# Two bottleneck blocks on one core: rows of the 3x3 stage's first group later, bias on ScalarE, streams without a unit of look-ahead, more idle matmuls

## The chip, the cores and the metric

The kernel runs on one core of a Trainium2 chip. The metric is the device time of one execution in microseconds (us). Three executions of the kernel before took 1949.6, 1950.11 and 1950.57 us; the median, 1950.11 us, is what the change is compared with.

## The reference

Two residual bottleneck blocks, one after the other, on x of 64 images, 1024 channels, 14 x 14 pixels, all float32. One block is

```
out = relu(bn(conv1x1(x,   w1, b1), g1, be1))      # 1024 -> 256 channels
out = relu(bn(conv3x3(out, w2, b2), g2, be2))      # 256 -> 256, padding 1
out = bn(conv1x1(out, w3, b3), g3, be3)            # 256 -> 1024
out = relu(x + softplus(residual_scale) * out)
```

`bn` takes mean and variance of its own input over images and pixels. So each convolution has to be complete, as far as its statistics go, before what follows it can be scaled, and this cuts the kernel into stages.

## The kernel before

**Stages.** In the trace they stand as follows. First 1x1 convolution of block 0: to 304 us. 3x3 convolution of block 0: 305 to 589. Statistics of the last 1x1 convolution from a Gram matrix (`gram`): 589 to 672. A fused stage, last convolution of block 0 beside first of block 1 (`fused`): to 1270. 3x3 of block 1: 1271 to 1556. Its Gram matrix: to 1640. Last convolution of block 1 (`final`): to the end at 1951.

**Streams of 1x1 convolutions.** A 1x1 convolution is cut into units, each a seven-product scheme for a 2 x 2 block product (`class Seven`, methods `p1` to `p7`, each followed by `after1` to `after7`, which take the result out of PSUM). `stream` (line 300) yields the products in the order p1 of this unit, p3 and p4 of the unit before (`last`), then p6, p2, p5, p7. It keeps one unit in hand: `following = next(items, None)` at the top of the loop makes the next unit while this one is only starting. Making a unit has effects, since the generators that yield units also load x, make the sums that the products need, and send rows out. In `final.pairs` (lines 1157 to 1170) a pair of x tiles has four units (q = 0 to 3). At q = 0 `column_sums` makes four sums t3, t2, t1, t4 on VectorE (lines 430 to 433; t1 and t2 have one buffer each, t3 and t4 two). After each unit the unit two back goes out: `go_out` (line 520) does one row on VectorE (line 522) and starts two transfers on SyncE's queue (line 525). After q = 1 the next two x tiles are loaded on the same queue (line 123) into a pool of five tiles. `Conv3.add` (line 466) adds a product to x on VectorE. p3 accumulates into the bank that p5 wrote, so it must wait until `after5`'s add of line 466 has read that bank.

**The 3x3 stage.** `conv2` (line 556) works in eight groups of eight images. Rows are combined first (VectorE makes combinations of input rows: `combine`, lines 658 to 723), then per combination columns are combined and multiplied. A group has six combinations in the pairs (1, 2), (3, 4), (5, 0); I number them as items 0 to 47, so item 6 opens the second group. An item needs from VectorE `sums` (line 624), `v` (line 630) and `diffs` (line 640), each made once for a pair, and has on TensorE, in the order of the loop at line 963: `m` from `sums` (`start`), the odd half of the `columns` of the item before, `l` from `diffs` (`middle`), the even half of its own `columns` from `v`. ScalarE copies m into the `columns` banks (lines 758 and 760) and l into `ls` (line 768). `outputs` adds `columns` and `ls` on VectorE (line 801). The very first item has no m; its bias comes in by four scalar_tensor_tensor operations in `add_to` (line 799). `finish` (line 811) is a generator that is sent every finished item: after the fourth item of a group it makes `c` and `e` (lines 835, 836) and writes the group's output rows: six operations of `stt` (line 593) and one add (line 843). In group 0 `begin` (line 901) then takes a mean of some rows as the centre of later moments (lines 905 to 908). The item three ahead is made only after `finish` was sent the current one.

**What sets the order.** The text is traced once. A planner lays down each engine's instructions by when they can run in its own simulated time; among those that can run, the one traced earlier goes first. It reaches far ahead for what is ready: the t3 of line 430 at 1706.25 us is traced at the start of the unit that runs at about 1719. `keep_in_program_order` pins an instruction behind the one traced just before it on its engine; all matmuls, ScalarE's `act` calls and line 522 are pinned. [...]

**Idle matmuls.** `busy` (line 170) issues matmuls of 448 columns whose result nobody reads; six of them stand at the end of each 3x3 stage (line 979), ahead of the Gram stage's first transposes (`by_tensor`, line 1030).

Of the kernel before, what the change touches and what calls it, by code (L numbers as in the profile page):

```python
# [87 lines left out]
def bottlenecks(ctx: ExitStack, tc: tile.TileContext, x, w1s, w2s, w3s, pars, out):  # L88
# [81 lines left out]
    def busy(psum, tag, n, with_=None):  # L170

        v = ident if with_ is None else with_
        for i in range(n):
            matmul(psum.tile(448, tag), v, v[:, :1].to_broadcast([P, 448]), start=True, stop=True)
# [122 lines left out]
            yield from self.p3()  # L297
            yield from self.p4()

    def stream(items, beside=lambda: None):  # L300


        before, items = None, iter(items)
        now = next(items)
        while now is not None:
            following = next(items, None)
            yield from now.p1()
            if before is not None:
                beside()
                yield from before.last()  # L310
                beside()
            else:
                yield from now.p2()
            yield from now.p6()
            if before is not None:
                before.end()
                if following is not None:
                    beside()
                    yield from now.p2()
            beside()  # L320
            yield from now.p5()
            beside()
            yield from now.p7()
            beside()
            if following is None:
                yield from now.p2()
            before, now = now, following
        yield from before.last()
        before.end()

# [225 lines left out]
    def conv2(psum, pool, b, par, aff, affine_of, stats):  # L556
# [35 lines left out]
        def stt(to, a, by, c):  # L592
            return nc.vector.scalar_tensor_tensor(to, a, by, c, ALU.mult, ALU.add)
# [131 lines left out]
        class Products:  # L725
# [36 lines left out]
            def middle(self):  # L762

                l = self.whole("l", DIFF, self.diffs)
                ls = pool.tile([P, 2 * MS * RT * GI * WH], FP, tag="ls", name="ls", bufs=BUFS["ls"])
                self.ls = ls[:, : 2 * MS * self.n].rearrange("p (q o n) -> p q o n", q=2, o=MS)
                for q, sign in (EVEN, 1.0), (ODD, -1.0):
                    nc.scalar.activation(self.ls[:, q], l, AF.Copy, scale=sign)

            def columns(self, *qs):  # L770
                parts = {ODD: [(D3M1, self.r[:, :, :, WH:])], EVEN: [(D0M2, self.r[:, :, :, :WH])]}
# [20 lines left out]
            def add_to(self, f):  # L792

                to, v, ls = halves(f), self.by_columns(self.banks), self.by_columns(self.ls)
                if self.first:
                    for q, o in itertools.product((EVEN, ODD), range(MS)):
                        one = [w[:, q].rearrange("p (o l) c -> p o l c", o=MS)[:, o] for w in (to, v, ls)]
                        bias = par[:, B2 + o : B2 + o + 1]
                        nc.vector.scalar_tensor_tensor(one[0], one[1], bias, one[2], ALU.add, ALU.add)
                else:  # L800
                    nc.vector.tensor_add(to, v, ls)  # L801
                return f

        def halves(f):
# [3 lines left out]
        def outputs(c):  # L808
            return c.add_to(new("f", c.lines // GI))

        def finish():


            for g in range(NG):
# [9 lines left out]

                ca = yield
                fa = outputs(ca)
                fb = outputs((yield))
                a, d = new("fa"), new("fb")
                nc.vector.tensor_add(a, fa, fb)
# [11 lines left out]
                if by_transfer:  # L841

                    nc.vector.tensor_add(out_rows[0][:, :, :full], a3, c)
                    nc.scalar.activation(out_rows[0][:, :, full], a[:, :, full], AF.Copy)
                else:
                    nc.vector.tensor_add(a3, a3, c)
                end = y_grp[:, :, g, H - 1]
                if by_transfer:

                    for o in range(MS):  # L850
                        stt(out_rows[3][:, o], e[:, o], 8.0, d3[:, o])
                    nc.scalar.activation(end, d[:, :, full], AF.Copy)
                else:
                    stt(d3, e, 8.0, d3)
# [108 lines left out]
        for k in range(NG * NF):  # L963
# [25 lines left out]
    def gram(psum, pool, homes, aff, minus_c, beside):  # L989
# [162 lines left out]
    def final(psum, pool, xpool, xs, a, w3, aff):  # L1152


        units = []

        def pairs():
            for t in range(1, T - 1, 2):
                ys = [[two(t + i, s) for i in range(2)] for s in range(MS)]
                sums = column_sums(pool, ys, PX)  # L1160
                for q in range(CS // 2):
                    units.append(Conv3Pair(psum, pool, xs[t : t + 2], q, PX, ys, sums, w3, aff, out[t : t + 2]))
                    yield units[-1]
# [12 lines left out]
        residual(psum, xs[T - 1], 1, T - 1, a, aff)  # L1176

    def fused(psum, pool, xpool, xs, w1, w3, aff, par, stats, one_done):
# [17 lines left out]
        a, c = stream(first_convs()), stream(last_convs())  # L1196
        for i in range(LAG):
            next(c)
        while True:
# [125 lines left out]
    with tc.tile_pool(name="first", bufs=1) as one, tc.tile_pool(  # L1325
# [35 lines left out]
        for _ in stream(items(), beside):  # L1361
            pass

    for b in range(2):
# [95 lines left out]
```

## Time and profile before

| | us |
|---|---|
| median of three executions | 1950.11 |
| the profiled execution | 1952.81 |
| its span, first to last instruction | 1951.0 |
| TensorE busy in the span (matmuls) | 1918.5 |
| VectorE busy | 1541.4 |
| ScalarE busy | 1044.6 |
| GpSimd busy | 577.1 |

The profiled execution is 1.8 us longer than its span and 2.7 us longer than the median. Busy times of TensorE are of matmuls that overlap in a pipeline. By stage, VectorE was busy 12 to 17 of 20 us in the first stage, 19 to 20 of 20 us in the 3x3 stages, 13 to 15 of 20 in the fused stage and about 16 of 20 in the last one; TensorE shows 20.00 of 20 us nearly throughout, but for the joints of the stages, one gap in each 3x3 stage and a small gap in every pair of the last stage.

### The profile page before, as it was taken

The page shows a single profiled execution, that of the slowest core. Times are in us where ns is not written, and L with a number is a line of the kernel's source. Part 1 is how long each engine was busy: PE and PEld are TensorE (multiplying, and loading weights), DVE is VectorE, ACT ScalarE, POOL GpSimd, SP SyncE. Part 2 cuts the span into 40 slices and gives each one's busy share as a digit, 9 for nine tenths or more (in the row PEclk, how much of TensorE's full clock was granted, in tenths as well). Part 3 has the DMA queues.
Part 4 walks back from the last instruction along what each step waited for, and adds up shares of the span by engine and source line. Part 5 has one row for each costly group of instructions (what it writes and reads, how often), then busy time and mean ns, then how long its engine had stood idle before and what let it go on. Part 6 is the DMA issues. An engine that isn't in the chain of part 4 may idle for free.

```text
span 1951.0 us, 27071 instructions
## 1 busy us (share of the span) xinstructions
PE 1918.5 (98%) x9430; PEld 1617.1 (83%) x9430; DVE 1541.4 (79%) x2479; ACT 1044.6 (54%) x2094; POOL 577.1 (30%) x674
## 2 busy tenths in 40 slices
PE   9999999999999999999999999989999999999998
PEld 5555558999997799999999999989999887555555
DVE  5778768999997667676776776699999975888786
ACT  2222214677765155555555555457777642666665
POOL 0111100212105133433433433201121061666664
PEclk9999999999999999999999999999999999999999
DMA  7777634787848534444444444268787386899997
GB/s 290 277 250 256 242 120 162 190 227 202 228 140 213 190 149 182 166 168 183 178 166 165 183 181 166 100 183 216 209 218 220 125 204 234 296 324 341 332 341 265
DMA packets 201849, 413.92 MB, mean 212 GB/s; under 512 B 37808, under 2 KB 178000, under 8 KB 185200
## 3 DMA queue, kind: packets, MB, share of 16 engines
q1 hardware_dynamic: 161728, 324.66, 48.8%
q0 software_dynamic: 34368, 36.45, 9.2%
q10 hardware_dynamic: 5616, 51.06, 6.3%
q8 instruction: 75, 1.23, 0.3%
q14 instruction: 62, 0.51, 0.1%
HBM read 263.75 MB, written 115.34 MB: 194 GB/s over the span
## 4 chain that ended last, share of the span: by engine, by line
PE 88%; DVE 5%; issue 5%; ACT 1%; POOL 1%; DMA 1%; SPq 0%; DVEq 0%; POOLq 0%; ACTq 0%
PE cy L168 16%; PE columns L168 14%; PE ay L168 14%; PE cp L168 12%; PE ap L168 9%; PE l L168 7%; PE m L168 7%; PE cx L168 4%; PE ax L168 4%; PE ps L168 1%; DVE x L466 1%; POOL u L215 1%; DVE ct L431 1%; DMA u<-y 0%; DVE ct L433 0%
## 5 line engine op out<-in xcount | busy, mean ns | idle before, releaser
L333 ACT ACTIVATE cu<-cy,scale 128x196 f32<-128x196 f32 (+1 forms) x552 | 257.7, 473 | 286.6 <-PE cy L168 280.0
L168 PE MATMUL columns<-v,ub 128*128 128x224 f32 (+1 forms) x1536 | 301.7, 338 | 0.0
L168 PEld LDWEIGHTS columns<-v,ub 128*128 128x128 f32 x1536 | 270.4, 189 | 3.1
L333 ACT ACTIVATE x<-x,shift 128x392 f32<-128x392 f32 x428 | 239.6, 612 | 55.4 <-POOL x L492 53.4
L466 DVE SCALAR_TENSOR_TENSOR x<-cp,scale,x 128x196 f32<-128x196 f32 (+1 forms) x368 | 178.3, 485 | 97.9 <-PE cp L168 96.3
L168 PE MATMUL cy<-ct,ws 128*128 128x196 f32 (+1 forms) x736 | 221.9, 383 | 1.1 <-ACT cu L333 1.1
L487 POOL TENSOR_TENSOR x<-x,cu 128x196 f32<-128x196 f32 (+1 forms) x184 | 158.9, 864 | 173.9 <-ACT cu L333 162.4
L168 PE MATMUL ay<-at,ws 128*128 128x196 f32 (+1 forms) x752 | 209.1, 381 | 0.0
L492 POOL TENSOR_TENSOR x<-x,cu 128x392 f32<-128x392 f32 x124 | 125.9, 1015 | 193.2 <-DVE x L466 183.5
L168 PEld LDWEIGHTS ay<-at,ws 128*128 128x128 f32 x752 | 136.5, 190 | 33.4
L168 PEld LDWEIGHTS cy<-ct,ws 128*128 128x128 f32 x736 | 133.4, 190 | 36.4 <-ACT cu L333 3.8
L168 PE MATMUL m<-sums,ua 128*128 128x224 f32 (+1 forms) x752 | 148.3, 341 | 5.4 <-DVE sums L624 5.4
L513 POOL TENSOR_TENSOR x<-x,cu 128x392 f32<-128x392 f32 x120 | 124.5, 1039 | 86.1 <-DVE x L466 65.4
L168 PE MATMUL l<-diffs,ub 128*128 128x224 f32 (+1 forms) x768 | 148.9, 337 | 0.0
L168 PEld LDWEIGHTS m<-sums,ua 128*128 128x128 f32 x752 | 132.9, 191 | 7.2 <-DVE sums L624 6.5
L333 ACT ACTIVATE au<-ay 128x196 f32<-128x196 f32 (+1 forms) x141 | 53.7, 381 | 156.0 <-PE ay L168 153.2
L466 DVE SCALAR_TENSOR_TENSOR x<-cx,scale,x 128x196 f32<-128x196 f32 (+1 forms) x184 | 89.4, 486 | 59.0 <-PE cx L168 57.9
L168 PEld LDWEIGHTS l<-diffs,ub 128*128 128x128 f32 x768 | 134.5, 189 | 0.8 <-issue 0.4
L867 POOL DMA_DIRECT2D y<-f x24 | 30.9, 1529 | 349.5 <-DVE f L801 309.0
L168 PE MATMUL cx<-y,w 128*128 128x196 f32 (+1 forms) x404 | 124.1, 392 | 0.4 <-DVE x L1141 0.4
L168 PE MATMUL cy<-y,w 128*128 128x196 f32 (+1 forms) x404 | 123.8, 392 | 0.0
L168 PE MATMUL cp<-zt 128*128 128x257 f32 x392 | 118.9, 385 | 1.7 <-DVE zt L1041 1.7
(214 smaller groups left out, 4001.7 us busy)
## 6 DMA issues: line engine op xcount, KB each, us to landing
x<-in_x SPq DMA_DIRECT2D x62, 1568.0 KB, 6.8
ub<-u SPq DMA_DIRECT2D x94, 768.0 KB, 5.4
x<-mid SPq DMA_DIRECT2D x32, 1568.0 KB, 8.6
mid<-x ACTq DMA_DIRECT2D x31, 1568.0 KB, 5.1
out<-x SPq DMA_DIRECT2D x123, 392.0 KB, 6.6
ua<-u SPq DMA_DIRECT2D x94, 256.0 KB, 3.0
u<-y POOLq DMA_DIRECT2D x48, 256.0 KB, 6.1
home<-y SPq DMA_DIRECT2D x90, 96.0 KB, 4.2
```

Of the source, the lines that this page charges most:

```text
L168: tc.keep_in_program_order(nc.tensor.matmul(*args, **kw))
L215: nc.gpsimd.dma_start(out=us[b][i][:, s, o], in_=u)
L333: tc.keep_in_program_order(nc.scalar.activation(*args, **kw))
L431: nc.vector.tensor_add(t2, t3, ys[0][0])
L466: nc.vector.scalar_tensor_tensor(v, bank, self.scale[:, o : o + 1], v, ALU.mult, ALU.add)
L487: nc.gpsimd.tensor_add(self.part(1, 1), self.part(1, 1), u3)
L492: nc.gpsimd.tensor_add(v, v, self.u12)
L513: nc.gpsimd.tensor_add(v, v, self.u12[:, i * self.n : (i + 1) * self.n])
L867: nc.gpsimd.dma_start(out=out_rows[3][:, o], in_=fa[:, o, :full], accum_op=ALU.add)
```

## The change

Six edits. In code:

```diff
-    def stream(items, beside=lambda: None):
-        before, items = None, iter(items)
-        now = next(items)
-        while now is not None:
-            following = next(items, None)
+    def stream(items, total, beside=lambda: None):
+        before = None
+        for k, now in enumerate(items, 1):
             yield from now.p1()
...
-                if following is not None:
+                if k < total:
                     beside()
                     yield from now.p2()
...
-            if following is None:
+            if k == total:
                 yield from now.p2()
-            before, now = now, following
+            before = now
...
                 for q, sign in (EVEN, 1.0), (ODD, -1.0):
-                    nc.scalar.activation(self.ls[:, q], l, AF.Copy, scale=sign)
+                    if self.first:
+                        for o in range(MS):
+                            bias = par[:, B2 + o : B2 + o + 1]
+                            nc.scalar.activation(self.ls[:, q, o], l[:, o], AF.Identity, bias=bias, scale=sign)
+                    else:
+                        nc.scalar.activation(self.ls[:, q], l, AF.Copy, scale=sign)
...
-                if self.first:
-                    for q, o in itertools.product((EVEN, ODD), range(MS)):
...
-                        nc.vector.scalar_tensor_tensor(one[0], one[1], bias, one[2], ALU.add, ALU.add)
-                else:
-                    nc.vector.tensor_add(to, v, ls)
+                nc.vector.tensor_add(to, v, ls)
...
                 fa = outputs(ca)
+                if g == 1:
+                    begin(y_grp[:, :, 0, 1 : 4 * full : 4, :])
...
-                for o in range(MS):
-                    stt(out_rows[1][:, o, :full], e[:, o], 2.0, d3[:, o])
-                    stt(out_rows[2][:, o], c[:, o], 4.0, a3[:, o])
...
-                if g == 0:
-                    begin(out_rows[1][:, :, :full])
+                def complete():
...
+                if g:
+                    complete()
...
                 fa = outputs((yield))
+                if g == 0:
+                    complete()
...
-        busy(psum, "m", 6)
+        busy(psum, "m", 7)
...
                 yield by_tensor(a if a < head else a + STEP)
+                if i == 0:
+                    busy(psum, "ax", 1)
...
-        for _ in stream(pairs()):
+        for _ in stream(pairs(), (T // 2 - 1) * CS // 2):
```

`complete` holds the row operations of lines 838 to 854, unchanged. A unit is now made when its turn comes, that is, after p7 of the unit before; the other calls of `stream` get their number of units in the same way. The row operations of group 0 stand after the outputs of the group's fifth item; in the other groups they stay. The first item's bias goes into `ls` by four activations instead of two. The centre is made in group 1, after the outputs of item 6, from the same rows of group 0.

More of the change, by code (lines that the diff above doesn't have):

```diff
@@ L794, in add_to @@
                 to, v, ls = halves(f), self.by_columns(self.banks), self.by_columns(self.ls)
-                if self.first:
-                    for q, o in itertools.product((EVEN, ODD), range(MS)):
-                        one = [w[:, q].rearrange("p (o l) c -> p o l c", o=MS)[:, o] for w in (to, v, ls)]
-                        bias = par[:, B2 + o : B2 + o + 1]
-                        nc.vector.scalar_tensor_tensor(one[0], one[1], bias, one[2], ALU.add, ALU.add)
-                else:
-                    nc.vector.tensor_add(to, v, ls)
+                nc.vector.tensor_add(to, v, ls)
                 return f
@@ L837, in finish @@
                 a3, d3 = (v[:, :, :full] for v in (a, d))
-                for o in range(MS):
-                    stt(out_rows[1][:, o, :full], e[:, o], 2.0, d3[:, o])
-                    stt(out_rows[2][:, o], c[:, o], 4.0, a3[:, o])
[L841 to L846, printed above, removed]
                 end = y_grp[:, :, g, H - 1]
-                if by_transfer:
+                def complete():
                     for o in range(MS):
[L851 to L854, printed above, removed]
-                if g == 0:
-                    begin(out_rows[1][:, :, :full])
+                        stt(out_rows[1][:, o, :full], e[:, o], 2.0, d3[:, o])
+                        stt(out_rows[2][:, o], c[:, o], 4.0, a3[:, o])
+                    if by_transfer:
+                        nc.vector.tensor_add(out_rows[0][:, :, :full], a3, c)
+                        nc.scalar.activation(out_rows[0][:, :, full], a[:, :, full], AF.Copy)
+                    else:
+                        nc.vector.tensor_add(a3, a3, c)
+                    if by_transfer:
+                        for o in range(MS):
+                            stt(out_rows[3][:, o], e[:, o], 8.0, d3[:, o])
+                        nc.scalar.activation(end, d[:, :, full], AF.Copy)
+                    else:
+                        stt(d3, e, 8.0, d3)
+                if g:
+                    complete()
                 if last_group:
@@ L1194, in first_convs @@
                 yield Conv1(psum, pool, xs[t : t + 1], (t,), w1, par, stats, one_done)
-        a, c = stream(first_convs()), stream(last_convs())
+        a, c = stream(first_convs(), T), stream(last_convs(), (T - 1) * CS // 2)
         for i in range(LAG):
@@ L1359, in items @@
                 yield Conv1(psum, one, xs, (t, t + 1), w1, par[0], stats1, one_done)
-        for _ in stream(items(), beside):
+        for _ in stream(items(), T // 2 - 1, beside):
             pass
```

## The prediction

> **What bounds the kernel.** I read the page's first two parts, then the waits of TensorE, then the busy times of all engines in windows around each wait, and last the timeline there.
>
> ```profile
> span 1951.0 us, 27071 instructions
> PE 1918.5 (98%) x9430; PEld 1617.1 (83%) x9430; DVE 1541.4 (79%) x2479; ACT 1044.6 (54%) x2094; POOL 577.1 (30%) x674
> ...
> PE cp L168 <- DVE x L466: 7.0, 15, 0.9
> PE m L168 <- DVE sums L624: 5.4, 2, 2.7
> ```
>
> TensorE (PE) is the bound: 32.5 us of the span are without a matmul. The last two lines, from the waits (total, times, longest), are the largest of what VectorE causes. So a gain can only come from gaps of TensorE, or from stretches in which its clock is halved. The windows show those (columns: stretch, its length, busy us of PE, PEld, DVE, ACT, POOL, granted clock, DMA share, GB/s):
>
> ```profile
> 344.00:346.00 2.00, 0.00 (x0) 0.00 (x0) 2.00 (x4) 0.61 (x2) 0.80 (x1) 1.00 0.17 64
> 346.00:348.00 2.00, 1.98 (x7) 1.86 (x8) 2.00 (x2) 0.00 (x0) 2.00 (x3) 0.69 0.55 55
> 348.00:350.00 2.00, 2.00 (x7) 1.76 (x7) 2.00 (x2) 1.20 (x3) 1.06 (x1) 0.50 1.15 117
> ...
> 1558.00:1560.00 2.00, 2.00 (x9) 1.61 (x10) 1.85 (x3) 2.00 (x2) 0.00 (x0) 0.62 0.00 0
> 1560.00:1562.00 2.00, 2.00 (x10) 1.82 (x10) 1.21 (x2) 2.00 (x3) 0.23 (x1) 0.53 0.00 0
> ```
>
> VectorE is full while TensorE stands still at 344, and then the clock is 0.5. Three places are left to work out.
>
> **First, group 0 of the 3x3 stage.** The timeline (start, duration, engine, line):
>
> ```profile
> 338.57 0.51 DVE L593 SCALAR_TENSOR_TENSOR y<-fc,fa 128x336 f32<-128x336 f32 x1
> ...
> 341.85 0.92 DVE L905 BATCH_NORM_STATS2 first_stats<-y 128x6 f32<-128x336 f32 x2
> 342.68 0.18 DVE L907 BATCH_NORM_AGGREGATE mv_first<-first_stats 128x2 f32<-128x6 f32 x1
> 342.76 1.07 DVE L688 TENSOR_TENSOR r<-steps 128x896 f32<-128x896 f32 x1
> ...
> 344.86 1.10 DVE L624 TENSOR_TENSOR sums<-r 128x896 f32<-128x896 f32 x1
> 345.87 1.77 DVE L630 TENSOR_TENSOR v<-r 128x1536 f32<-128x1536 f32 x1
> ...
> 346.02 2.68 PE L168 MATMUL m<-sums,ua 128*128 128x224 f32 x8 [2.69 <-DVE sums L624]
> ```
>
> Rows (338.57 to 341.85, 3.28 us) and centre (about 1.3 us) stand ahead of item 6's last row combination and `sums`. TensorE is free for m(6) at 343.3 and waits 2.69 us. The halved clock then makes m and `columns` take 4.82 us to the next start (350.84) where 3.05 is usual: 1.77 us more. Lost: 4.46 us. In block 1 the rows are the same (wait 2.68; 7.49 instead of 3.05 us from free to l, so 4.44).
>
> After the change, by starts in the list: the last row combination at 338.57 (1.00), one row operation in the hole before its result (0.42), sums 1.00 until 341.0, outputs of item 4 1.00, the other rows 2.86 until 344.9, then v 1.66 and diffs 1.00 until 347.6. m(6) starts at 343.3 with no wait, `columns` follows, and l(6) could start at 346.4 but needs diffs: **the wait moves to l and is 1.3 us**. l(6) starts at 347.65 instead of 350.84, 3.2 us earlier.
>
> Whether 1.3 us halves the clock decides 1.8 us. The nearest row: before 1271.44 TensorE idled 1.82 us, and another 1.42 before 1276.12, and the windows there show 1.00. [...] For 1.3 us I follow the row of 1.82: full clock.
>
> What is late next is l(12) in group 1. From the end of diffs(6), 348.63, to that of diffs(12), 383.50, VectorE takes 34.87 us, 2.1 of them idle; the centre adds 1.3. If 1.1 us of idleness (waits for ScalarE and for its own results) stay, it is 35.2, if none, 34.1; TensorE needs 33.5 from l(6) to l(12) and would wait 0.6 to 1.7. An order with v and sums placed otherwise gives 0.2. I take 0.6. From group 3 on, sums lead their m by 7 us, so nothing more is lost: 2.6 us a block, **5.2 us**; ends 0 (all given back in group 1) and 8.9 (no wait left).
>
> The bias: four operations of line 799 (1.45 us by starts) become one add of 1.00. ScalarE has four activations of 128x224 for two of 128x448: 1.78 (row of line 758) for 0.98. Sums(2) ends at 321.56 and m(2) starts at 321.61, so an add in one piece ahead of it costs up to 0.4, and a shorter list gains 0.45. Counted 0; ends -0.9 and +0.9 for both blocks. The moments that wait for the centre start at 367.08 on ScalarE, after item 6's outputs (357.19) plus 1.3: hidden.
>
> **Second, the last stage.** In every pair:
>
> ```profile
> 1702.80 0.83 DVE L431 TENSOR_TENSOR ct<-ct,y 128x392 f32<-128x392 f32 x1
> 1703.66 0.57 DVE L433 TENSOR_TENSOR ct<-y,ct 128x392 f32<-128x392 f32 x1
> 1704.14 0.62 DVE L466 SCALAR_TENSOR_TENSOR x<-cx,scale,x 128x392 f32<-128x392 f32 x1
> 1704.68 0.56 DVE L432 TENSOR_TENSOR ct<-y 128x392 f32<-128x392 f32 x1
> 1705.15 0.62 DVE L466 SCALAR_TENSOR_TENSOR x<-cp,scale,x 128x392 f32<-128x392 f32 x1
> ...
> 1705.83 0.93 PE L168 MATMUL cp<-y,ws 128*128 128x392 f32 x2 [0.44 <-DVE x L466]
> ```
>
> The next pair's sums (lines 431, 433, 432) precede the add that reads p5's bank, and p3 waits for it. A pair takes 19.13 us (1686.69 to 1705.83), while 56 matmuls at 0.329 are 18.44: 0.69 us lost, 14 times, 9.7 us.
>
> Without look-ahead the sums are traced after both adds. Line 431 may still go at 1702.80 (nothing else can run); then come the add of p2 and, at 1704.1, that of p5, done by 1704.7, before p3 at 1705.23. The sums have room: t2 is needed at p6, two products after p3.
>
> [...]
>
> But two more things move by a unit (4.61 us): `go_out`, with its VectorE row and two transfers, and the two x loads. SyncE's queue waits at line 123 for "DMA out<-x" (28.8 us in 16 waits), so loads start when the rows two units back have landed. Now they start at 1715.56, 11.0 us after the pair's p1 at 1704.57; less the stall and plus a unit, at 14.9. The first load lands 6.3 to 7.4 us later (minimum and median), at 21.2 to 22.3. Its tile is needed by the add after the next pair's p5, 18.44 + 3.95 = 22.4, and TensorE notices 0.65 later (p7 and p1 are between, less the add). **Slack falls from some 4.7 us to about 1.** The DMA has 6.42 MB a pair: 336 GB/s now, 348 at 18.44 us; the windows show up to 352. So I count 0.5 of the 0.69 us: **7.0 us**; ends 0 and 9.7. At the end of the kernel rows go out a unit later, but the last transfer is that of the last tile at 1947.88: nothing.
>
> **Third, the clock at the Gram stage.** Block 1's first transposes start at 1556.58 after 1.22 us of idleness, with 0.67 more between the first two, and the clock is halved from 1558.5 to 1562; block 0 has the same gaps and 1.00. From first transpose to the last products of the Gram matrix it is 74.60 us against 73.89: 0.7, and at the fourth transpose 0.8. An idle matmul takes 0.78 us (4.69 for six). The seventh fits into the 1.22, the other between two transposes (1.29 from start to start, 0.44 for four transposes): no more than 0.1 late. **0.8 us**; ends 0 and 1.6 (both blocks).
>
> **Elsewhere.** In the first stage loads are set by the release of tiles (SyncE at line 123 waits for PE ap 649.9 us in 41 waits, over the kernel), not by their place in the text; the fused stage has TensorE at 20.00 of 20 and VectorE idle 0.24 before its line 431 at 787.56. Both 0; if a sum came late in each of 31 tiles by 0.1, 3 us.
>
> **Sum.** 5.2 + 7.0 + 0.8 = 13.0 us. Against the profiled execution 1952.8 - 13.0 = 1939.8; it is 2.7 above the median, so the forecast for the median is 1937.
>
> **Rivals.**
> 1. The rows only move the wait: group 1 gives all of the first step back. For: VectorE is at 18.8 to 20 of 20 us until 380. Against: 2.1 us of its idle time. 13.0 - 5.2 = 7.8: 1942.
> 2. The loads take the place of the sums in the last stage: TensorE loses 0.69 a pair as before. For: the slack of 1. 13.0 - 7.0 = 6.0: 1944.
> 3. Slower: the same loads, later still. One that lands 8.2 us after its start begins to stall p3, at 8.9 it costs the old 0.69, beyond 9.3 the kernel is slower. Second loads land after 10.8; a first load like that stalls 2.65 us: (2.65 - 0.69) x 14 = 27, less 6: 1971. Against: first loads of 6.3 to 7.4.
> 4. The planner finds the same order, since it goes by what is ready and not by place: no change, 1950. Against: the row operations of group 0 stand by their place today.
>
> **From this to numbers.** Forecast case 0.60, its own range 1931 to 1942 (ends of the three places, not all at once). Rival 1: 0.12; rival 2: 0.13; rival 3: 0.07; rival 4: 0.08. The range 1930 to 1946 holds the first three but for a tenth, leaving out 3 and 4. The bound for "same" is 0.2%, 3.9 us, about what a measurement of this kernel can tell from no change. Faster 0.83, same 0.09, slower 0.08.
>
> **What would show it.** Right: no wait of m for sums of 2.7 us, in its place one of l for diffs near 1.3 and clock 1.00 at 346; the wait of cp for line 466 gone from the last stage, pairs of 18.4 to 18.6 us; clock 1.00 at the Gram stage of block 1. Wrong: waits of line 466 for x loads, pairs above 19.1, a halved clock near 347, or waits of l in group 1 as long as those won in group 0.

## The result and the profile after

The changed kernel takes **1944.43 us** (median of 9 executions, 1943.94 to 1944.92); the kernel before, run beside it, 1950.57 (median of 9, 1949.38 to 1952.90). The ratio is 0.9966, interval 0.9955 to 0.9976: about 6.1 us faster. That lies inside the wide range of 1930 to 1946, outside the forecast case's own range of 1931 to 1942, and 7.4 us above the forecast of 1937. The two profiled executions differ by more, 1952.81 against 1944.06, 8.7 us. Why these two differences are not the same is part of the answer.

The page of the changed kernel begins:

```profile
span 1942.3 us, 27081 instructions
...
PE 1918.6 (99%) x9438; PEld 1612.1 (83%) x9438; DVE 1544.3 (80%) x2473; ACT 1046.2 (54%) x2098; POOL 575.1 (30%) x674
```

TensorE's busy time by the page is within 0.1 us of that before (1918.5), and the time without a matmul has fallen from 32.5 to 23.7 us. Its waits (total, times, longest) now read:

```profile
PE l L168 <- PE columns L168: 2.6, 4, 0.9
...
PE m L168 <- DVE sums L622: 1.5, 4, 0.6
...
PE cp L168 <- DVE x L464: 0.9, 1, 0.9
```

The 15 waits of cp for the add (7.0 us) have become one, and the two waits of m of 2.7 us have become four of at most 0.6; new are four short ones of l. The windows that showed the halved clock (stretch, length, busy PE, PEld, DVE, ACT, POOL, granted clock, DMA share, GB/s):

```profile
344.00:346.00 2.00, 2.00 (x12) 1.98 (x11) 2.00 (x3) 0.83 (x2) 1.36 (x2) 1.00 0.77 160
346.00:348.00 2.00, 1.09 (x7) 0.77 (x6) 2.00 (x3) 0.86 (x3) 1.21 (x1) 1.00 0.73 161
...
1558.00:1560.00 2.00, 0.57 (x5) 0.35 (x3) 1.92 (x4) 2.00 (x3) 1.50 (x2) 1.00 0.20 47
```

The clock is 1.00 in all of them, as it is in the whole execution. The timeline of the 3x3 stage (start, duration, engine, line):

```profile
343.42 1.67 PE L168 MATMUL m<-sums,ua 128*128 128x224 f32 x8
...
344.68 1.75 DVE L628 TENSOR_TENSOR v<-r 128x1536 f32<-128x1536 f32 x1
...
346.35 1.09 DVE L638 TENSOR_TENSOR diffs<-r 128x896 f32<-128x896 f32 x1
...
347.53 1.75 PE L168 MATMUL l<-diffs,ub 128*128 128x224 f32 x8 [0.91 <-PE columns L168]
```

m(6) starts without a wait and l(6) starts at 347.53 behind `diffs`. (The wait is put down to `columns`, which ended long before; the end of `diffs` at 347.44 is what l(6) follows.)

Where the time went, stage by stage, from the first matmul of a stage to that of the next (a Gram stage counts to the start of its own last matmul, the last stage from there to the end of the span), in us:

| stage | before | after | difference | forecast |
|---|---|---|---|---|
| 3x3, block 0 | 284.87 | 282.89 | -1.98 | -2.6 |
| 3x3, block 1 | 285.13 | 283.53 | -1.60 | -2.6 |
| Gram stage, block 0 | 71.43 | 71.87 | +0.44 | 0 |
| Gram stage, block 1 | 72.15 | 71.33 | -0.82 | -0.8 |
| last stage | 322.30 | 317.64 | -4.66 | -7.0 |
| all else | 915.14 | 915.02 | -0.12 | 0 |

So 8.7 of the forecast's 13.0 us. The missing 2.3 us of the last stage are seen in its timeline. TensorE no longer shows an idle time there, because matmuls overlap in the trace (one lasts 0.49 us, and the next starts 0.329 after it), but it still starts late: products start 0.66 us apart, but p3 (cp from y) comes 0.77 us after p1 (1718.65 to 1719.42) and, one unit later, 0.70 (1723.48 to 1724.18). VectorE's lines there, with p3 and GpSimd's add between them:

```profile
1716.87 0.83 DVE L429 TENSOR_TENSOR ct<-ct,y 128x392 f32<-128x392 f32 x1
1717.73 0.57 DVE L431 TENSOR_TENSOR ct<-y,ct 128x392 f32<-128x392 f32 x1
1718.22 0.62 DVE L464 SCALAR_TENSOR_TENSOR x<-cx,scale,x 128x392 f32<-128x392 f32 x1
...
1718.76 0.62 DVE L464 SCALAR_TENSOR_TENSOR x<-cp,scale,x 128x392 f32<-128x392 f32 x1
...
1719.29 0.93 DVE L520 TENSOR_SCALAR x<-x,shift 128x392 f32<-128x392 f32 x1
1719.42 0.93 PE L168 MATMUL cp<-y,ws 128*128 128x392 f32 x2
1719.95 1.14 POOL L485 TENSOR_TENSOR x<-x,cu 128x392 f32<-128x392 f32 x1
1720.14 1.37 DVE L430 TENSOR_TENSOR ct<-y 128x392 f32<-128x392 f32 x1
...
1721.43 0.55 DVE L428 TENSOR_TENSOR ct<-y 128x392 f32<-128x392 f32 x1
...
1723.52 0.61 DVE L464 SCALAR_TENSOR_TENSOR x<-cp,scale,x 128x392 f32<-128x392 f32 x1
```

Lines 428 to 431 are t3, t2, t1, t4. t2 **and t4** still stand ahead of the adds of p2 and p5; the add of p5 ends at 1719.38, and p3 follows at 1719.42. Then go_out's row, t1 (1.37 us where it usually takes 0.56) and the t3 of a later pair come, and the adds behind them are late once more at 1724.18. VectorE has no idle time from t2 to that last add, 7.3 us. In starts of matmuls (0.329 us apart when nothing waits) the first stall costs 0.13 us, and 0.10 more until the next start; the second 0.04 and 0.10: 0.37 a pair, 18.81 us instead of the 18.44 without any. Before it was 19.13.

### The profile page after: what moved, and what is told of

The parts are those of the page before. It is cut to its first block, busy times and chain, and to the rows that moved or that the text cites. A ratio compares the mean times of both kernels' runs of the same rounds, so it can differ in the third digit from the quotient of the medians.

```text
span 1942.3 us, 27081 instructions
## 1 busy us (share of the span) xinstructions
PE 1918.6 (99%) x9438; PEld 1612.1 (83%) x9438; DVE 1544.3 (80%) x2473; ACT 1046.2 (54%) x2098; POOL 575.1 (30%) x674
## 4 chain that ended last, share of the span: by engine, by line
PE 92%; DVE 5%; DMA 1%; ACT 1%; issue 1%; SPq 0%; POOL 0%; DVEq 0%; ACTq 0%
PE cy L168 17%; PE ay L168 17%; PE columns L168 13%; PE cp L168 12%; PE ap L168 10%; PE m L168 6%; PE l L168 6%; PE cx L168 5%; PE ax L168 4%; PE ps L168 1%; DMA home<-y 1%; ACT y L544 1%; DVE v L628 0%; DVE sums L622 0%; DVE steps L697 0%
## 5 line engine op out<-in xcount | busy, mean ns | idle before, releaser
L168 PE MATMUL cp<-y,ws 128*128 128x196 f32 (+1 forms) x368 | 113.6, 390 | 0.9 <-DVE x L464 0.9
```

The lines of the kernel that those rows point to most:

```text
L168: tc.keep_in_program_order(nc.tensor.matmul(*args, **kw))
```

## The experiments

My theory on reading this was: the last stage is short of its forecast because VectorE's sums still crowd at the pair's boundary; the 3x3 stage because group 1 takes back most of what group 0 gives, and most of the gain is the clock; and the clock is halved in only a part of the executions, so its 4 us may not be counted in full against a median. The rivals were the transfers, a part of the change that takes something back, and another order that would give more. Beside each kernel the kernel before ran on the same chip. In the table, lengths of the stages are from the one profiled execution, and a star marks a stage in which the trace shows the clock at 0.50; the ratio is to the kernel before that ran beside it.

| run | 3x3 b0 | 3x3 b1 | Gram b0 | Gram b1 | last | median | ratio, interval |
|---|---|---|---|---|---|---|---|
| before | 284.87* | 285.13* | 71.43 | 72.15* | 322.30 | | |
| streams alone | 284.68* | 283.47 | 72.05* | 72.17* | 317.91 | 1947.63 | 0.9980, 0.9972 to 0.9988 |
| 3x3 part alone | 282.90 | 283.52 | 71.54 | 71.89 | 322.31 | 1949.34 | 0.9990, 0.9984 to 0.9997 |
| idle matmuls alone | 284.87* | 285.14* | 71.57 | 71.66 | 322.33 | 1951.04 | 0.9997, 0.9989 to 1.0005 |
| before, t2 with two buffers | 283.28 | 283.47 | 71.81* | 71.82 | 320.58 | 1949.86 | 0.9989, 0.9981 to 0.9998 |
| changed | 282.89 | 283.53 | 71.87 | 71.33 | 317.64 | 1944.43 | 0.9966, 0.9955 to 0.9976 |
| + rows of group 1 later | 282.89 | 283.52 | 71.93 | 71.43 | 317.65 | 1944.38 | 0.9968, 0.9955 to 0.9980 |
| + t4 written later | 282.89 | 283.52 | 71.44 | 71.33 | 317.65 | 1944.61 | 0.9967, 0.9955 to 0.9980 |
| + row by ScalarE | 282.89 | 283.53 | 71.55 | 71.81 | 318.26 | 1944.74 | 0.9968, 0.9957 to 0.9980 |
| + no u3 in the last unit | 282.89 | 283.52 | 71.98 | 71.33 | 317.98 | 1944.08 | 0.9966, 0.9953 to 0.9978 |
| + t4 pinned | 282.88 | 283.50 | 71.54 | 71.73 | 315.84 | 1942.33 | 0.9955, 0.9942 to 0.9967 |
| + t4 pinned, no u3 | 282.89 | 283.50 | 71.44 | 71.70 | 313.97 | 1941.44 | 0.9950, 0.9937 to 0.9962 |
| the same, fewer transfers | 282.87 | 283.51 | 71.46 | 71.70 | 312.17 | 1938.93 | 0.9938, 0.9924 to 0.9952 |
| changed, fewer transfers | 282.88 | 283.50 | 71.47 | 71.54 | 317.30 | 1944.04 | 0.9963, 0.9951 to 0.9976 |
| + bias by VectorE | 282.94 | 283.22 | 71.41 | 71.36 | 317.55 | 1943.94 | 0.9960, 0.9948 to 0.9973 |
| + t4 pinned, bias by VectorE | 282.93 | 283.21 | 71.86 | 71.75 | 316.23 | 1942.46 | 0.9951, 0.9937 to 0.9964 |

### The change in three parts

The streams alone, on the kernel before (in `stream` and where it is called):

```diff
-    def stream(items, beside=lambda: None):
+    def stream(items, total, beside=lambda: None):
...
-            following = next(items, None)
...
```

> The kernel before with the streams' part of the change alone (no unit taken ahead); rows, bias, centre and idle matmuls as before. Theory (the last stage gave 4.7 of the 7.0 us that were counted, because VectorE's adds are still late twice in a pair): the pair of the last stage takes 18.81 us, the last stage 317.6, and the time is 4.7 us below the kernel before, so 1945.9. Rival (the streams gave the 7.0 us, and another part of the change took 2 to 3 back): a pair of 18.6, 1943.6. The first and the fused stage stay as they are by both (305.0; 0 us). In the 3x3 stage m still waits 2.69 us for sums in both blocks; if the halved clock near 346 is a thing of single executions, it may be missing here at one or both of these waits; if it follows from the wait, it is there both times (granted clock 0.50 for 3.4 us).

The 3x3 stage alone (rows by `complete`, bias in the activations, `begin` in group 1):

```diff
...
+                if g == 1:
+                    begin(y_grp[:, :, 0, 1 : 4 * full : 4, :])
...
+                if g == 0:
+                    complete()
...
```

> The kernel before with the 3x3 stage's part alone (rows of group 0 an item later, bias by ScalarE, centre in group 1). Theory (three quarters of what these places lost was the halved clock, which the kernel before has only in a part of its executions; of the wait itself group 1 takes most back): the traces give 1.98 and 1.60 us, 3.6 together, of which 3.5 are the clock; so the time is 1 to 3 us below the kernel before, 1947.5 to 1949.5, with l(6) waiting 0.9 us and m(12) with l(12) some 0.6 to 1.0 us together. Rival (the prediction's term): 5.2 us, 1945.3, with all of it there against each run of the kernel before. The Gram stage may or may not show the halved clock.

The idle matmuls alone:

```diff
-        busy(psum, "m", 6)
+        busy(psum, "m", 7)
...
+                if i == 0:
+                    busy(psum, "ax", 1)
```

> The kernel before with the two edits to the idle matmuls alone (seven instead of six ahead of the Gram stage, one more between two transposes). Theory: these hold the clock at 1.00 at the Gram stage, worth 0.8 us in an execution in which it would have been halved and nothing in the others: 0 to 0.8 us below the kernel before, 1949.8 to 1950.6, and no clock below 1.00 after the transposes of either block. Rival (the clock is halved at the Gram stage whatever the idle matmuls do): 0.50 there in a block, and no gain. At 346 and 1313 the clock is free to be halved or not, as in the streams' run.

Against 1951.56 us for the kernel before that ran beside them, the parts are worth 3.9, 2.2 and 0.5 us: 6.7 together, as the whole is worth 6.1 within its interval. The streams give 4.4 us of the last stage, with the same two stalls and 18.81 us a pair; nothing else took their gain back. (In one pair of this run an add starts at 1896.20, right after its x load landed at 1896.02, and p3 comes 0.37 us later than in the other pairs: the loads have little room already.) The 3x3 part gives 2.2 us and not 5.2.

What the 3x3 part is made of shows in the stages with and without a star. The wait of m for `sums` of 2.7 us was there in both blocks of all four kernels that keep the old order of rows. The clock fell in five of these eight waits. These are the same windows of the run with the streams alone,

```profile
346.00:348.00 2.00, 1.77 (x5) 1.63 (x6) 2.00 (x3) 0.00 (x0) 2.00 (x3) 0.50 0.41 41
...
1312.00:1314.00 2.00, 0.64 (x3) 0.64 (x4) 2.00 (x4) 0.00 (x0) 0.48 (x1) 1.00 0.00 0
1314.00:1316.00 2.00, 2.00 (x13) 1.99 (x12) 2.00 (x3) 0.79 (x2) 2.00 (x3) 1.00 0.34 33
```

halved after the wait in block 0, not after the equal wait in block 1, and of the kernel before with another buffer, where it is halved in neither:

```profile
344.00:346.00 2.00, 0.00 (x0) 0.00 (x0) 2.00 (x4) 0.60 (x2) 0.80 (x1) 1.00 0.17 63
346.00:348.00 2.00, 1.98 (x10) 1.98 (x11) 2.00 (x2) 0.17 (x1) 2.00 (x3) 1.00 0.55 55
```

Without the star the old order takes 283.28 and 283.47 us, with it 284.87 and 285.13. The changed kernel takes 282.89 and 283.53. So the edits of this stage, rows and bias together, are worth 0.39 us in block 0 and nothing in block 1; the rest, 1.6 us in each block, is the halved clock, and it is there to be won only in the executions that have it. The 78 executions of the kernel before that ran beside all these experiments agree, by the mean clock of each: 4 with 0.999 took 1949.35 us on average, 33 with 0.998 took 1950.63, and 41 with 0.997 took 1952.22. None has 1.000. The profiled execution of the prediction (0.997, 1952.81 us) is of the slowest kind. The changed kernel's 1944.43 is 4.9 us below the first four, about what the profiles give without any halved clock (4.66 for the last stage, 0.39 for the 3x3 stage). The run of the idle matmuls alone keeps the stars of the 3x3 stage and has none in the Gram stage.

### Is it the rows' order, or VectorE's work?

First, the rows of group 1 an item later as well:

```diff
-                if g:
+                if g > 1:
                     complete()
...
-                if g == 0:
+                if g < 2:
                     complete()
```

> The changed kernel, with the rows of group 1 put down a combination later too, as group 0's are. Theory (the rows and the centre only hand the wait on to the next group, because VectorE has little idle time until group 2): m(12) and l(12) wait no more (0.22 and 0.41 us in block 0, 0.57 and 0.41 in block 1), and l(16) or l(18), which had 2.1 and 0.3 us in hand, wait some tenths; the 3x3 stage falls from 282.89 and 283.53 by 0.2 to 0.8 us in each block, so the time is 0.4 to 1.6 us below the changed kernel. Rival (VectorE has the room, only the order was wrong): all of 0.63 and 0.98 us is won. Second rival (group 2 takes all): no change in the stage. Clock 1.00 throughout[...]. The last stage stays at 18.81 us a pair.

No gain; the stage is as the second rival has it. The timeline (TensorE, and the `diffs` of VectorE that l(12) needs) of the changed kernel at item 12 of block 0,

```profile
378.46 1.78 PE L168 MATMUL m<-sums,ua 128*128 128x224 f32 x8 [0.22 <-DVE sums L622]
...
380.99 1.09 DVE L638 TENSOR_TENSOR diffs<-r 128x896 f32<-128x896 f32 x1
...
382.18 1.75 PE L168 MATMUL l<-diffs,ub 128*128 128x224 f32 x8 [0.41 <-PE columns L168]
```

and of this run:

```profile
378.33 1.68 PE L168 MATMUL m<-sums,ua 128*128 128x224 f32 x8
...
382.43 1.75 PE L168 MATMUL l<-diffs,ub 128*128 128x224 f32 x8 [0.89 <-PE columns L168]
```

m(12) starts 0.38 us earlier and waits no more, and l(12) waits 0.48 us longer. Counted from the stage's first matmul (304.90 and 305.14) l(12) starts at 77.28 and 77.29 us. It was not group 2 that took it, as that rival said: l(12) itself did not move. (In block 1 l(12) waits 1.25 us instead of 0.41, and the clock stays at 1.00.) The other edit of the stage was taken back alone:

```diff
...
-                nc.vector.tensor_add(to, v, ls)
+                if self.first:
...
+                        nc.vector.scalar_tensor_tensor(one[0], one[1], bias, one[2], ALU.add, ALU.add)
```

> The changed kernel with the bias of the 3x3 stage's first item made by VectorE again (four operations instead of one add), rows and centre as changed. Theory (m(2) waits 0.39 and 0.28 us only because the one add of 1.00 us stands ahead of its sums, but l(6) and l(12) come when VectorE has done a fixed amount of work, so what is saved at m(2) is lost there): m(2) waits under 0.1 us, l(6) or l(12) wait longer by as much or up to 0.45 more (the four operations take 1.45 by starts), and the 3x3 stage stays within 282.8 to 283.4 and 283.4 to 284.0 us; time within 1 us of the changed kernel. Rival (the bias's edit costs its wait at m(2)): the stage falls by 0.39 and 0.28 us, 0.7 in all.

m(2) no longer waits, l(6) waits 1.33 instead of 0.91, and l(12) starts at 77.34. That is the theory in block 0: what is saved at m(2) is lost at l(6). In block 1 the stage falls by 0.3 us, near the rival's size, because m(12) waits 0.21 instead of 0.57. Starts from the stage's first matmul put the three orders side by side (block 0; the kernel before in an execution without the halved clock):

| | m(2) | l(6) | l(12) |
|---|---|---|---|
| old order | 16.60 | 44.15 | 77.67 |
| changed | 17.07 | 42.64 | 77.28 |
| changed, bias by VectorE | 16.60 | 42.69 | 77.34 |

The change brings l(6) forward by 1.5 us, and 1.1 of it is gone at l(12), with either form of the bias. VectorE sets the time: l(12) starts 0.10 us after `diffs` ends (382.08), and from the end of the `diffs` of l(6) to there VectorE takes 34.65 us in block 0 of the changed kernel and of both these runs. It is not all work: 1.28 us of it are idle, 1.03 in one wait for `columns` (at 359.66 in the changed kernel).

### What holds p3 in the last stage

The kernel before, with the second buffer of t4 given to t2:

```diff
-            v = pool.tile([P, n], FP, tag=f"ct{i}", name=f"ct{i}", bufs=2 if i > 1 else 1)
+            v = pool.tile([P, n], FP, tag=f"ct{i}", name=f"ct{i}", bufs=2 if i in (1, 2) else 1)
```

> The kernel before, look-ahead and all, with the second buffer taken from t4 and given to t2 (sums of lines 431 and 433; same memory). t2 is then free two units earlier, and t4 can only be made after p4 of the pair before, so neither stands ahead of the adds of p2 and p5; t1 (0.56 us) still does. Theory (the order on VectorE, here set by when the sums' buffers come free, makes p3 late; transfers don't): the 0.69 us a pair shrink to 0.1 to 0.3, the pair to 18.5 to 18.8, and the time falls by 5 to 8 us, to 1943 to 1945.5, without any change to the streams. Rival (only the look-ahead lets sums stand ahead of the adds; the buffers are no matter): a pair of 19.0 to 19.13, within 1.5 us of the kernel before. Second rival (x loads or go_out bound the pair): the same 19.1, with waits of line 466 for loads.

A miss: a pair takes 19.05 us, 1.1 less in 14 pairs. The stall of 0.69 us at the boundary shrinks to 0.15, but one of 0.47 appears at the next unit's p3. It was the first sign that the order within VectorE's stretch only chooses where TensorE loses. Then, on the changed kernel, t4 was written later in the text:

```diff
-        nc.vector.tensor_sub(t4, ys[1][0], t2)
+        if with_t4:
+            nc.vector.tensor_sub(t4, ys[1][0], t2)
...
+        def after6(self):
+            super().after6()
+            if self.o[0] == 0:
+                nc.vector.tensor_sub(self.t4, self.b[1][0], self.t2)
...
```

> The changed kernel with t4 of the last stage (line 431 after the change) written with p6 of the pair's first unit instead of with the other sums. Theory (at the pair's boundary t4 stands ahead of the adds of p2 and p5 on VectorE, which makes the add of p5 end at 1719.4 where p3 could start at 1719.3): if the planner then puts it behind these adds, the first stall of a pair (0.13 and 0.10 us) goes, the second (0.04 and 0.10) stays, since t4 still falls into the same stretch: a pair of 18.58, 3.2 us less than the changed kernel. If the planner puts it ahead of the adds again, all is as in the changed kernel: 18.81. Rival (transfers or another engine make p3 late): 18.81 with t4 behind the adds.

The planner put t4 where it had been, directly behind t2, since it goes by what is ready; so this run, at 18.81 us a pair, decides nothing. (It also says that the place in the text, to which the prediction gave weight, does not keep a sum behind an add.) Next, go_out's row by ScalarE:

```diff
-            tc.keep_in_program_order(nc.vector.tensor_scalar(v, v, self.shift[:, o : o + 1], 0.0, ALU.add, ALU.max))
+            act(v, v, AF.Relu, bias=self.shift[:, o : o + 1])
```

> The changed kernel with the row of go_out (line 520 after the change, 0.81 to 0.93 us of VectorE in each unit) made by ScalarE, which is busy for 13.8 of 20 us there. Theory (VectorE is busy without a break for 7.3 us over two units at each pair's boundary, and the adds at its end are late by 0.1 to 0.2): without 1.8 us of it both stalls go, a pair takes 18.44 to 18.5, the last stage 312.6 to 313.3, 4.5 to 5.2 us less than the changed kernel. Rival (loads, or the Pool's adds, or ScalarE): the pair stays at 18.8 or gets longer, with waits for cu of line 331 if it is ScalarE.

A miss: 18.84 us in most pairs. The first stall stays, and I should have seen it, because the row stands behind the add of p5. The second goes, but a product of that unit, p6, now starts 0.07 and 0.10 us late (1688.31), right after a copy of ScalarE to cu (1687.69 to 1688.26): ScalarE, with the rows added, has become the late one there. Two adds, at 1837.07 and 1856.18, also wait for x loads (0.28 and 0.48 us). And GpSimd's part, with u3 left out in a pair's last unit:

```diff
+        def after7(self):
+            if self.o[0] < CS // 2 - 1:
+                super().after7()
```

> The changed kernel, in which the last of the four units of a pair of the last stage leaves out u3: neither its activation nor its add by GpSimd (line 485) is made, so one eighth of the rows of the output lacks that term. Theory (t1 takes 1.37 us instead of 0.56 because it starts while GpSimd's add of u3 runs, 1719.95 to 1721.09, and goes on only when that ends): t1 takes 0.56 us, the second stall of a pair (0.04 and 0.10 us at 1724.18) goes, the first stays: a pair of 18.66, 2.1 us less than the changed kernel. Rival (t1 is long for another reason, such as its place behind line 520): 1.37 us, and 18.81.

VectorE's timeline of this run, at the boundary:

```profile
1701.89 0.55 DVE L430 TENSOR_TENSOR ct<-y 128x392 f32<-128x392 f32 x1
```

t1 takes 0.55 instead of 1.37, the second stall is gone and the first is not: 18.66 us a pair, as expected. But the kernel is not faster. The last pairs lose 0.43, 0.75 and 0.42 us at p3, of a kind that the changed kernel does not have: two of the adds ahead of them wait 1.06 and 1.05 us for an x load, and the third starts at 1893.40, right after its load landed at 1893.22. Then t4 was pinned behind the adds:

```diff
-        nc.vector.tensor_sub(t4, ys[1][0], t2)
+        tc.keep_in_program_order(nc.vector.tensor_sub(t4, ys[1][0], t2))
```

> The changed kernel with t4 of each pair pinned in the order of the text, which puts it behind the adds of p2 and p5, go_out's row and t1. Theory (VectorE's unbroken chain from t2 to the add before the second unit's p3, 7.3 us, is what is too long; its order within only says where TensorE loses): the first stall (0.13 and 0.10 us) goes, TensorE is 0.23 earlier at the second, and the second grows from 0.04 and 0.10 to about 0.27 and 0.10; a pair of 18.7 to 18.8, 0 to 1.5 us below the changed kernel. Rival (only t4's place was wrong): the second stall stays as it is, a pair of 18.58 and 3.2 us less. Second rival (transfers are the bound already): 18.8, with the stalls as waits for loads.

The timeline of this run around the second unit:

```profile
1719.25 0.55 DVE L430 TENSOR_TENSOR ct<-y 128x392 f32<-128x392 f32 x1
...
1719.72 1.38 DVE L431 TENSOR_TENSOR ct<-y,ct 128x392 f32<-128x392 f32 x1
...
1723.10 0.61 DVE L464 SCALAR_TENSOR_TENSOR x<-cp,scale,x 128x392 f32<-128x392 f32 x1
...
1723.77 0.93 PE L168 MATMUL cp<-y,ws 128*128 128x392 f32 x2
```

The first stall is gone, the second has grown to 0.15 and 0.10 (the theory said 0.27 and 0.10): 18.69 us a pair, and 1942.33 us. It is 2.1 us below the changed kernel's median, beside 1.8 us less in the last stage of the profiles (315.84 against 317.64), and no complete version was lower; the intervals of the two ratios overlap. It is now t4 that starts during GpSimd's add (1719.25 to 1720.68) and takes 1.38, and t1, which starts as the add does, that takes 0.55: the length goes with the place, not with the sum.

### What comes after the sums

Here both stalls are taken away by the last two edits together (t4 pinned, and u3 left out in a pair's last unit), first with every transfer and then with fewer. The code is the edit for fewer transfers, which leaves out the rows of a pair's second image:

> t4 pinned as in the run before, and u3 of a pair's last unit left out (one eighth of the output's rows lacks that term), so that t1 meets no add of GpSimd. Theory with both limits (first VectorE's chain, then the transfers: 6.42 MB a pair at the 344 GB/s of the fullest windows are 18.66 us): both stalls go, the first pairs take 18.44 us, and after some pairs p3 waits for adds that wait for x loads, 0.4 to 0.8 us each; the last stage takes some 317 to 318, as long as in the run without u3, so leaving the sums' stalls out altogether is worth less than 1 us. Rival (the transfers have room, as the forecast's term of 7.0 us took it): 18.44 in all 14 pairs, last stage 312.6 to 313.3.

```diff
-            for i in range(2):
+            for i in range(1):
                 nc.sync.dma_start(
```

> The run before, and go_out sends only the rows of the first of a pair's two images out in the 14 pairs (a quarter of the last stage's transfers; the second images of the output are left out). Theory with both limits: 18.44 us in all 14 pairs, no wait for loads, DMA at 250 to 265 GB/s, last stage 312 to 313.5, 4 to 5 us less than the run before. Rival (something other than the transfers makes the late p3 of the run without u3): the same waits and 317 to 318.

The first pairs take 18.44 us, as both theories have it. After ten pairs, VectorE and TensorE of the run with every transfer show:

```profile
1852.09 0.62 DVE L464 SCALAR_TENSOR_TENSOR x<-cp,scale,x 128x392 f32<-128x392 f32 x1 [1.26 <-DMA x<-mid]
...
1852.77 0.93 PE L168 MATMUL cp<-y,ws 128*128 128x392 f32 x2 [0.63 <-DVE x L464]
```

The add waits 1.26 us for the x load, p3 0.63 for the add. In the next pair the add at 1870.89 starts 0.08 us after its load has landed, and those at 1889.42 and 1908.03 wait again for loads (0.46 and 0.54). The windows of this run, and then of the one with fewer transfers:

```profile
1820.00:1840.00 20.00, 20.00 (x62) 11.59 (x61) 15.87 (x26) 12.81 (x24) 12.41 (x13) 1.00 1.00 351
1840.00:1860.00 20.00, 19.37 (x59) 10.94 (x58) 14.83 (x25) 12.58 (x24) 11.88 (x12) 1.00 0.96 338
```

```profile
1820.00:1840.00 20.00, 20.00 (x62) 11.54 (x61) 15.83 (x27) 12.83 (x24) 12.40 (x13) 1.00 0.78 264
1840.00:1860.00 20.00, 20.00 (x63) 11.51 (x62) 15.81 (x26) 13.42 (x26) 11.98 (x12) 1.00 0.80 268
```

With 264 to 268 GB/s no pair waits, and the stage takes 312.17 us, 1.80 less; with every transfer the DMA is full (its share is 1.00 and 0.96). A pair at 18.44 us asks for 348 GB/s (6.42 MB), and the engines move 338 to 351. The theory's limit was right in kind, and too strict in size: the stage took 313.97, not 317 to 318, because the loads' slack lasts for ten pairs. The counter-test on the changed kernel itself, the same edit:

> The changed kernel itself with the rows of only the first of a pair's two images sent out by go_out (the second images of the output are left out). Theory (in the changed kernel as it is, the sums on VectorE are the limit of the last stage, and the transfers only the next one): the pair stays at 18.81 us with the two stalls where they are, last stage 317.0 to 317.7, time within 0.7 us of the changed kernel. Rival (the transfers are the limit already): stalls shrink, last stage 313 to 316.

18.81 us a pair, with both stalls where they were. In the changed kernel as it stands the sums are the limit, not the transfers.

Last, t4 pinned and the bias by VectorE:

> The version with t4 pinned, and the bias by VectorE again. Theory: the two edits act in different stages; last stage 315.84 as with t4 pinned alone, 3x3 stage as in the run before, so 1942.3 plus 0 to 0.9. Rival: 0.7 less than with t4 pinned alone, 1941.6. Either is below both kernels.

1942.46 us, nothing more than with t4 pinned alone, and one add at 1835.83 already waits 0.42 us for a load. Near 1942 the complete kernel touches the transfers.

## Why the prediction was off

The direction, the three places and most of the mechanisms were right. The sum was 13.0 us where the profiled executions differ by 8.7 (4.3 us off), and the shift from the profiled execution to the median added 3.1.

**Last stage: 7.0 us counted, 4.66 measured. The step that failed is "Line 431 may still go at 1702.80 (nothing else can run); then come the add of p2 and, at 1704.1, that of p5, done by 1704.7".** Not only t2 went ahead but t4 behind it, which is ready as soon as t2 is; the place in the text did not hold it. "The sums have room" failed too: t1 takes 1.37 us beside GpSimd's add, 0.55 in the run without that add. The trace before already showed this in t3, and I did not read it:

```profile
1706.07 1.13 POOL L487 TENSOR_TENSOR x<-x,cu 128x392 f32<-128x392 f32 x1
1706.25 1.37 DVE L430 TENSOR_TENSOR ct<-y 128x392 f32<-128x392 f32 x1
```

Together the two steps cost 0.37 us a pair where the term left 0.19. Rivals 2 and 3, the loads, are refuted for the changed kernel (no add in its profile waits for a load, and fewer transfers shorten the stage by 0.34 us only). That the median lies at the 1944 that rival 2 named is chance. The fear was sound, though: slack is gone at 18.44 us a pair. The full 9.7 us of that place, its upper end, were not to be had with all transfers: even without any stall from the sums the stage took 313.97, 8.3 less than before.

**3x3 stage: 5.2 counted, 3.58 between the profiles.** The first half was right: l(6) at 347.53 (forecast 347.65), a wait of 0.91 (1.3), clock 1.00. The term mis-sized was "I take 0.6" for l(12), from a span of 0.6 to 1.7: from l(6) to l(12) TensorE took 34.65 us instead of 33.5, so 1.1, and in block 1 34.99, so 1.5. The hope behind 0.6 was that VectorE's idleness would go; 1.28 us of it stayed. The bias, "counted 0", is nothing in block 0 and costs 0.3 in block 1.

**The clock, and the median.** "The halved clock then makes m and `columns` take 4.82 us" was read from one execution and taken as a property of the kernel. It is one of the execution. Rival 1 (the rows only move the wait) is nearly the truth about the wait: 0.4 us remain in block 0 and none in block 1. The gain is the clock's, and it was then counted in full *and* the 2.7 us by which the profiled execution exceeds the median were taken off as well. An execution longer than the median because its clock was halved must not be corrected twice; the profiled execution after is at 1944.06 and its median at 1944.43. With 1939.8, the forecast without that shift, the miss is 4.6 us instead of 7.4.

**The Gram stage: 0.8 counted; 0.82 in block 1, 0.4 net.** The +0.44 of block 0 is scatter: without the halved clock, block 0 takes 71.41 to 71.98 us over the runs. The match in block 1 is in part luck for the same reason: it takes 72.15 and 72.17 us with the halved clock, and 71.33 to 71.89 without. Idle matmuls alone are 0.5 us, with an interval that includes none. In all profiles with these matmuls, the Gram stages have full clock; of the eight Gram stages without them four have a star.

Rival 4 (the planner finds the same order) fell for the change, but describes well what it did to t4.

## What to carry to other kernels

A loss that comes and goes between executions, like the halved clock here (1.6 us, after five of the eight waits of 2.7 us), is worth its price times the share of executions that pay it, and it explains the distance from median to profile, so it may be counted once only. Where an engine works without a break for some microseconds around a boundary, add up its whole stretch to the next deadline, not only what stands ahead of the first one; reordering mostly shifted the stall here (from 0.37 to 0.25 us a pair), and a shorter stretch as well (t1 at 0.55 us instead of 1.37, without GpSimd's add) removed it. Before counting the last tenths of such a stall, look at what is next: here the DMA share was 1.00 (1820 to 1840 us) at the very pace that the forecast assumed, 18.44 us a pair.

## What the hardware showed

**VectorE's sums and rows took longer beside GpSimd's adds.** t1 starts at 1720.14, GpSimd's add runs from 1719.95 to 1721.09, and t1 ends 0.42 us after that, in 1.37 us; in the run without that add t1 takes 0.55. In all 14 pairs t2 and t1 start during such an add and end 0.42 to 0.43 us after it; t2 takes 0.83 us in this way, where t4, which starts during none, takes 0.57. go_out's row (line 520, one tensor operand) shows the same: from 1660 to 1915 us all 54 rows start during an add of GpSimd and end 0.22 to 0.23 us after it, in 0.80 to 0.93 us. Three rows of the run without u3 take 0.41; the one at 1893.94 starts between two adds (one ends at 1893.17, the next starts at 1894.16). From these durations I estimate that some 1.6 of the 7.3 us of VectorE's stretch are lost in this way (0.26 of t2, 0.52 of the row, 0.82 of t1). The adds of line 464, of which one operand is in PSUM, take 0.61 us beside GpSimd's adds from 1722.60, and 0.62 at 1712.92, where no add of GpSimd runs.

**The halved clock lasted 3.41 us each time.** In the profile of the kernel before, the clock stands at 0.50 three times within the kernel, from 346.75, 1312.72 and 1558.48 us, for 3.413 us each; the starts lie 965.97 and 245.76 us apart, 283.0 and 72.0 times that length. The wait of m for `sums` of 2.7 us was followed by 0.50 in five of eight places, which cost 1.6 us, and by 1.00 in the other three. Nor does the length of the idle time tell the places apart at the other joints: 1.82 us without a matmul ahead of block 1's 3x3 stage left the clock at 1.00, while at the Gram stage 1.22 us and, between the first two transposes, 0.67 stood ahead of 0.50 in block 1 of the kernel before, and 1.22 and 0.66 ahead of 1.00 in block 0. What decides it was not shown.
